# Preparing the first block of an attention and experts kernel in another order: normalization by tiles, transposes between two weight halves, scores ahead of values

## The chip, the cores and the metric

The kernel runs on one core of a Trainium2 chip. The metric is the device time of one execution in microseconds (us), lower is better. TensorE (PE; PEld is its weight load) multiplies and transposes into PSUM. VectorE (DVE), ScalarE (ACT) and GpSimd (POOL) do the elementwise work, and SyncE (SP) issues most DMAs. Each engine works through a queue of its own, and semaphores order the queues against each other.

## What is computed

One layer with pre-normalization, in float32, on x of 4096 tokens by 256 features:

```
z  = layernorm(x)
x  = x + softmax(causal((z Qw) (z Kw)^T / 16)) (z Vw)
z1 = layernorm(x);  h = z1 W_in + b_in
route = the best 2 of 8 experts by softmax(h W_gate + b_gate), shares summing to 1
x  = x + (sum over experts of route * (relu(h W1 + b1) W2 + b2)) W_out + b_out
```

An expert has 1024 hidden features.

## The kernel before

The tokens are 8 blocks of 512 (`TB`), each of 4 tiles of 128 rows (`TPB`). Queries go in groups of 256 (`QB`), two for each block, 16 in all; group g needs the keys and values of groups 0 to g.

`prepare_scores` turns Qw and Kw by transposes on TensorE and multiplies them (L406, in two halves `pqk0` and `pqk1`, one for each 128 features), so that scores are z (Qw Kw^T) z^T; VectorE scales each half into `qk_sb` (L413). `stats0(b)` takes mean and variance of the four x tiles of a block on VectorE (L231, L232) and calls `ln_rstd`, which on GpSimd adds epsilon and raises to the power -1/2 (L237, L238) for four columns, one for each tile, at once. `ln_rows` computes the four shifts in one VectorE instruction (L244) and then four normalized tiles z (L251). `turn` transposes the four tiles on TensorE (L262, 8 transposes of 128x128 into two PSUM tiles of 128x512) and VectorE copies each PSUM tile to SBUF (L263). `turn` serves the first norm (`turn(0, ...)`, result zT) and the second (`turn(1, ...)` in `enter`, result z1T).

`project(b)` multiplies zT by the combined weights (L426, `pq`, copied to qT by VectorE, L433), and then makes the values (L438, `pv`, copied by ScalarE, L445). `scores(g)` multiplies zT by qT for each key group (L468), keeps the scores in SBUF (ScalarE, L477) and a running maximum (VectorE, L483). The last key group is masked (L487), the maximum over the keys is formed through the tiles `top` (L493 to L498), transposes `pt` (L504), a reduction `m` (L506) and transposes `pmax` (L511). VectorE subtracts it (L515, L521) and ScalarE takes the exponential (L518, L524). `attend(g)` multiplies by the values (L533, `po`), divides, adds to x, and takes the statistics of the second norm. `enter(b)` runs the second norm's transposes, multiplies by W_in (L280, `ph`) and adds biases on VectorE (L287, L288). `route(b)` picks the experts. The experts' work follows from about 520 us on. `prepare_biases` transposes biases and W_in and folds the gate into W_in (L179 to L217).

PSUM tiles come from three rotating sets: `ps_mm` (4 buffers: pqk, pq, ps, ph), `ps_tr` (2 buffers: pt, pmax, pz, the weights' transposes) and `ps_o` (2 buffers: pv, po). A tile waits until its buffer's last readers are done.

The order on each engine comes from a scheduler that starts from the order of the text and the dependencies; `tc.keep_in_program_order` fixes instructions against each other, and `tc.issue_after(i)` lets what stands under it follow i. At the start the text reads:

```
    stats0(0)
    ready = prepare_scores()
    first_rows = ln_rows(0, 0, attn)
    with tc.issue_after(ready.ins):
        turn(0, 0, first_rows, zT[0])
    ready = project(0)
    with tc.issue_after(ready.ins):
        stats0(1)
```

Some setup follows, then `prepare_biases()`, `row = scores(0)`, and the loop over the groups. In pass g the loop computes `scores(g + 1)` ahead of `attend(g)`; on the first group of a block it also runs `enter` for the block before, turns the next block and projects it.

Of the kernel before, what the change touches and what calls it, by code (L numbers as in the profile page):

```python
# [17 lines left out]
P = 128  # L18
# [17 lines left out]
def preln_attention_moe_kernel(  # L36
# [18 lines left out]
    nc = tc.nc  # L55

    _, S, D = x.shape
    NE, _, FF = W1.shape
    NT = S // P
    NB = S // TB  # L60
    TPB = TB // P
# [29 lines left out]
    def ps_mm(name):  # L91
        return psum.tile([P, TB], F32, tag="mm", name=name, bufs=4)

    def ps_tr(name):
        return psum.tile([P, TB], F32, tag="tr", name=name, bufs=2)
# [15 lines left out]
    for _ in range(5):  # L111
        done = nc.tensor.matmul(
            pw[:, :QB],
            lhsT=zeros,
            rhs=zeros.unsqueeze(1).to_broadcast([P, QB // P, P]),
            start=True,
            stop=True,
        )
# [40 lines left out]
    ident = const.tile([P, P], F32, tag="ident", name="ident")  # L159
# [17 lines left out]
    def prepare_biases():  # L177
        ptb = ps_tr("pbias")
        nc.tensor.transpose(ptb[:, :NBR], brows, ident[:NBR, :NBR])  # L179
        biasT = const.tile([P, NBR], F32, tag="biasT", name="biasT")  # L180
        nc.scalar.copy(biasT, ptb[:, :NBR])
        nc.sync.dma_start(
            out=bias1.rearrange("(e p) f -> p e f", p=P),
            in_=biasT[:, : NE * NF].rearrange("p (e f) -> p e f", f=NF),
        )

        winT = piece("winT", ND, D)
        for k in range(ND):
            pt = ps_tr(f"pwin{k}")
            for c in range(ND):  # L190
                nc.tensor.transpose(pt[:, ts(c, P)], win_sb[:, c, ts(k, P)], ident)
            nc.scalar.copy(winT[:, k, :], pt[:, :D])
        for c in range(ND):
            pg = ps_o(f"pwg{c}")
            for k in range(ND):
                nc.tensor.matmul(
                    pg[:, :NE],
                    lhsT=winT[:, k, ts(c, P)],
                    rhs=wgate_sb[:, k, :],
                    start=(k == 0),  # L200
                    stop=(k == ND - 1),
                )
            nc.vector.tensor_copy(win_sb[:, c, D:], pg[:, :NE])
        binc = piece("binc", ND, P)
        nc.vector.tensor_copy(
            binc, biasT[:, NE * NF :].unsqueeze(2).to_broadcast([P, ND, P])
        )
        pg = ps_o("pbg")
        for k in range(ND):
            nc.tensor.matmul(  # L210
                pg[:, :NE],
                lhsT=binc[:, k, :],
                rhs=wgate_sb[:, k, :],
                start=(k == 0),
                stop=(k == ND - 1),
            )
        nc.vector.tensor_tensor(bgate_bc, pg[:, :NE], bgate_bc, ALU.add)  # L217
# [3 lines left out]
    lns = [  # L221
        tuple(
            const.tile([P, NT, w], F32, tag=f"ln{k}{s}", name=f"ln{k}{s}")
            for s, w in (("mv", 2), ("rstd", 1), ("shift", 1))
        )
        for k in range(2)
    ]
# [3 lines left out]
        nc.vector.bn_stats(out=st, in_=xb[t // TPB][:, t % TPB, :])  # L231
        nc.vector.bn_aggr(out=lns[k][0][:, t, :], in_=st)  # L232

    def ln_rstd(k, b):
        s = ts(b, TPB)
        mv, rstd, _ = lns[k]
        nc.gpsimd.tensor_scalar_add(rstd[:, s, 0], mv[:, s, 1], EPS)  # L237
        nc.gpsimd.tensor_tensor(rstd[:, s, 0], rstd[:, s, 0], half[:, s], ALU.pow)  # L238

    def ln_rows(k, b, pool):  # L240

        s = ts(b, TPB)
        mv, rstd, shift = lns[k]
        nc.vector.scalar_tensor_tensor(  # L244
            shift[:, s, :], mv[:, s, 0:1], -1.0, rstd[:, s, :], ALU.mult, ALU.mult
        )
        zs = []
        for j in range(TPB):
            t = b * TPB + j
            z = pool.tile([P, D], F32, tag=f"z{k}", name=f"z{k}_{t}", bufs=TPB)  # L250
            nc.vector.tensor_scalar(  # L251
                z, xb[b][:, j, :], rstd[:, t, :], shift[:, t, :], ALU.mult, ALU.add
            )
            zs.append(z)
        return zs

    def turn(k, b, zs, zT):

        for c in range(ND):
            pt = ps_tr(f"pz{k}_{b}_{c}")  # L260
            for j in range(TPB):
                nc.tensor.transpose(pt[:, ts(j, P)], zs[j][:, ts(c, P)], ident)  # L262
            nc.vector.tensor_copy(zT[:, c, :], pt)  # L263


    share = [const.tile([P, NT], F32, tag=f"share{k}", name=f"share{k}") for k in range(TOPK)]
# [114 lines left out]
    attn = ctx.enter_context(tc.tile_pool(name="attn", bufs=1))  # L381
# [5 lines left out]
    zT = [attn.tile([P, ND, TB], F32, tag="kt", name=f"zT{b}", bufs=KT) for b in range(NB)]  # L387
# [2 lines left out]
    qk_sb = attn.tile([P, ND, D], F32, tag="qk", name="qk")  # L390
    qT = {}

    def prepare_scores():

        wT = {}
        for name, w in (("qwT", qw_sb), ("kwT", kw_sb)):
            wT[name] = attn.tile([P, ND, D], F32, tag=name, name=name)
            pt = ps_tr(f"p{name}")
            for h in range(ND):
                for c in range(ND):  # L400
                    nc.tensor.transpose(pt[:, ts(h * ND + c, P)], w[:, c, ts(h, P)], ident)
            nc.scalar.copy(wT[name].rearrange("p h d -> p (h d)"), pt)
        for c in range(ND):
            pp = ps_mm(f"pqk{c}")
            for h in range(ND):
                done = nc.tensor.matmul(  # L406
                    pp[:, :D],
                    lhsT=wT["qwT"][:, h, ts(c, P)],
                    rhs=wT["kwT"][:, h, :],
                    start=(h == 0),  # L410
                    stop=(h == ND - 1),
                )
            nc.vector.tensor_scalar_mul(qk_sb[:, c, :], pp[:, :D], QSCALE)  # L413
        return done

    def stats0(b):
        for t in range(b * TPB, (b + 1) * TPB):
            ln_stats(0, t)
        ln_rstd(0, b)

    def project(b):
        qT[b] = attn.tile([P, ND, TB], F32, tag="qT", name=f"qT{b}", bufs=2)
        for o in range(ND):
            pp = ps_mm(f"pq{b}_{o}")
            for c in range(ND):
                nc.tensor.matmul(  # L426
                    pp,
                    lhsT=qk_sb[:, c, ts(o, P)],
                    rhs=zT[b][:, c, :],
                    start=(c == 0),  # L430
                    stop=(c == ND - 1),
                )
            done = nc.vector.tensor_copy(qT[b][:, o, :], pp)  # L433
        nc.gpsimd.memset(vb[b][:, :, D : D + 1], 1.0)
        for j in range(TPB):
            pv = ps_o(f"pv{b}_{j}")
            for c in range(ND):
                nc.tensor.matmul(  # L438
                    pv[:, :D],
                    lhsT=zT[b][:, c, ts(j, P)],  # L440
                    rhs=vw_sb[:, c, :],
                    start=(c == 0),
                    stop=(c == ND - 1),
                )
            nc.scalar.copy(vb[b][:, j, :D], pv[:, :D])  # L445
        return done


    KU = QB // P
# [469 lines left out]

    stats0(0)
    ready = prepare_scores()
    first_rows = ln_rows(0, 0, attn)
    with tc.issue_after(ready.ins):
        turn(0, 0, first_rows, zT[0])
    ready = project(0)
    with tc.issue_after(ready.ins):
        stats0(1)
# [6 lines left out]
    first = const.tile([P, TPB, NE], F32, tag="first", name="first")  # L936
# [23 lines left out]
        in_=zero.unsqueeze(1).to_broadcast([P, TOPK * (TPB + 1), D]),  # L960
    )

    prepare_biases()
    row = scores(0)
    for g in range(NT // KU):
        b, q = divmod(g, QPB)
        coming = q == 0 and b + 1 < NB
        lg = []

        def send():  # L970
            lg.append(enter(b - 1, rows1, attn))


        last = q == 0 and b == NB - 1
        nxt = None
        if g + 1 < NT // KU:
            nxt = scores(g + 1, send if last else None)
        if coming:
            ahead = ln_rows(0, b + 1, attn)
        if last:  # L980

            early = seen
            tables["a"] = plan("a", early, NFULL, SB, 0)
            seen = route(b - 1, lg[0], seen, attn)
            got, hTs = {}, {}
            for n in range(AHEAD + 1):
                got[n] = fetch_rows(work[n])
            for n in range(AHEAD):
                got[n] += fetch_weights(work[n])
            weighed = AHEAD  # L990
        elif q == 0 and b > 0:
            send()
        if coming:
            turn(0, b + 1, ahead, zT[b + 1])
        attend(g, row)
        row = nxt
        if coming:
            project(b + 1)
        if lg and not last:
            seen = route(b - 1, lg[0], seen, attn)  # L1000
        if q == QPB - 1:
            ln_rstd(1, b)
            if b + 2 < NB:
                stats0(b + 2)
            rows1 = ln_rows(1, b, attn)
# [172 lines left out]
```

## Time and profile before

| | us |
|---|---|
| median of 3 runs | 1099.73 |
| the runs | 1099.19 to 1102.57 |
| the profiled execution's own time | 1095.71 |
| its span in the trace | 1093.9 |

| engine | busy, us | share of the span |
|---|---|---|
| TensorE | 1079.7 | 99% |
| VectorE | 691.7 | 63% |
| ScalarE | 331.9 | 30% |
| GpSimd | 236.9 | 22% |

The profile is one execution; its times are from its own start. A timeline line gives start and length in us, the engine, the line of the kernel, the operation, the tile written and the tiles read, the shape, how many instructions were merged, and in brackets the idle time of the engine just before and what ended it. A matmul of float32 shows as two records in the trace. The length of a merged matmul line includes the end of the last one, so that the next line can begin before it is over. PEclk is the TensorE clock that was granted, as a share of full speed.

### The profile page before, as it was taken

Reading aid. Unit: us, or ns where it says so; the run is one execution under the profiler, and the core shown is the slowest. Engines: PE = TensorE matmul, PEld = TensorE weight load, DVE = VectorE, ACT = ScalarE, POOL = GpSimd, SP = SyncE. Lnnn points to the kernel's source line nnn. Section 1 sums busy time; section 2 is a strip of 40 time slices with the busy share of each in tenths; the row PEclk is TensorE's granted clock in tenths of the full one; section 3 lists DMA queues with packets and bytes.
Section 4 is the critical chain, followed back from the end, with each engine's and each line's share of the span. In section 5 each row is a group of like instructions: output and inputs, shape, how many; then the busy total and the mean of one; then the engine's idle time right before and its main releaser. Section 6 shows DMA issues by size and latency. Waiting matters only on the chain.

```text
span 1093.9 us, 15689 instructions
## 1 busy us (share of the span) xinstructions
PE 1079.7 (99%) x5077; PEld 896.3 (82%) x5077; DVE 691.7 (63%) x2132; ACT 331.9 (30%) x730; POOL 236.9 (22%) x286
## 2 busy tenths in 40 slices
PE   8999999999999999999999999999999999999998
PEld 6778888888888888888888888686878777777887
DVE  4677576574574555536393743867678876767636
ACT  1223232332341423223132122232322332324244
POOL 2023211212011110201222332323232231313110
PEclk9999999999999999999999999999999999999999
DMA  8010101001001000100075456797979796969285
GB/s 267 1 39 1 40 0 40 1 1 39 1 0 40 1 1 1 39 1 19 21 255 170 141 170 215 248 309 236 326 228 336 240 336 217 327 220 320 96 289 191
DMA packets 114888, 148.34 MB, mean 136 GB/s; under 512 B 23149, under 2 KB 94770, under 8 KB 114804
## 3 DMA queue, kind: packets, MB, share of 16 engines
q1 hardware_dynamic: 105876, 129.70, 36.1%
q0 software_dynamic: 8384, 17.09, 4.6%
q8 instruction: 41, 0.67, 0.3%
q14 instruction: 43, 0.35, 0.2%
q10 hardware_dynamic: 544, 0.52, 0.1%
HBM read 124.79 MB, written 22.75 MB: 135 GB/s over the span
## 4 chain that ended last, share of the span: by engine, by line
PE 95%; DVE 3%; DMA 1%; POOL 0%; issue 0%; ACT 0%; SPq 0%; ACTq 0%; DVEq 0%
PE po L533 20%; PE ps L468 19%; PE pm_a L827 11%; PE pe_a L894 11%; PE pe_b L894 5%; PE pm_b L827 5%; PE ph L280 3%; PE pq L426 3%; PE pm_c L857 3%; PE pf L1064 3%; PE pv L438 3%; PE pe_c L894 3%; PE pe_d L894 2%; PE pm_d L857 2%; PE pz L262 1%; PE pm_z L827 1%
## 5 line engine op out<-in xcount | busy, mean ns | idle before, releaser
L533 PE MATMUL po<-v,s 128*128 128x257 f32 x1056 | 238.3, 381 | 0.7 <-ACT s L524 0.7
L468 PE MATMUL ps<-qT,zT 128*128 128x256 f32 x1088 | 233.1, 374 | 0.0
L468 PEld LDWEIGHTS ps<-qT,zT 128*128 128x128 f32 x1088 | 203.4, 191 | 26.9 <-DVE mx L483 0.4
L533 PEld LDWEIGHTS po<-v,s 128*128 128x128 f32 x1056 | 197.3, 191 | 27.3 <-issue 1.6
L477 ACT COPY s<-ps 128x512 f32<-128x512 f32 x120 | 70.2, 585 | 193.3 <-PE ps L468 153.9
L894 PE MATMUL pe_a<-w_a,mid_a 128*128 128x256 f32 x544 | 121.6, 381 | 0.0
L827 PE MATMUL pm_a<-hT_a,w_a 128*128 128x256 f32 x544 | 120.0, 379 | 0.0
L483 DVE TENSOR_TENSOR mx<-ps,mx 128x512 f32<-128x512 f32 x91 | 62.8, 690 | 88.7 <-ACT s L477 88.2
L894 PEld LDWEIGHTS pe_a<-w_a,mid_a 128*128 128x128 f32 x544 | 102.9, 190 | 18.7 <-issue 5.4
L356 POOL DMA_INDIRECT slots<-assign,ati x64 | 62.6, 978 | 256.2 <-DVE ati L354 238.1
L827 PEld LDWEIGHTS pm_a<-hT_a,w_a 128*128 128x128 f32 x544 | 103.6, 190 | 13.8
L836 ACT ACTIVATE mid_a<-pm_a,c_a 128x256 f32<-128x256 f32 x136 | 64.2, 472 | 165.2 <-PE pm_a L827 157.8
L518 ACT ACTIVATE s<-s 128x512 f32<-128x512 f32 x120 | 72.0, 629 | 51.2 <-DVE s L515 51.2
L794 DVE STREAM_TRANSPOSE hT_a<-h_a 32x128 f32<-32x128 f32 x272 | 82.2, 302 | 3.8
L515 DVE TENSOR_TENSOR s<-s,pmax 128x512 f32<-128x512 f32 x120 | 73.1, 682 | 8.2 <-PE pmax L511 8.2
L903 POOL DMA_INDIRECT parts<-y_a,slot_a x34 | 34.2, 1005 | 162.5 <-DVE y_a L902 132.5
L794 DVE STREAM_TRANSPOSE mid_c<-raw_c 32x256 f32<-32x256 f32 x128 | 55.8, 436 | 1.9
L894 PE MATMUL pe_b<-w_b,mid_b 128*128 128x256 f32 x256 | 56.8, 380 | 0.0
L827 PE MATMUL pm_b<-hT_b,w_b 128*128 128x256 f32 x256 | 56.6, 379 | 0.0
L894 PEld LDWEIGHTS pe_b<-w_b,mid_b 128*128 128x128 f32 x256 | 48.6, 190 | 9.3 <-issue 2.6
L827 PEld LDWEIGHTS pm_b<-hT_b,w_b 128*128 128x128 f32 x256 | 48.8, 190 | 6.5
L836 ACT ACTIVATE mid_b<-pm_b,c_b 128x256 f32<-128x256 f32 x64 | 30.1, 471 | 63.0 <-PE pm_b L827 63.0
(279 smaller groups left out, 1209.5 us busy)
## 6 DMA issues: line engine op xcount, KB each, us to landing
w_a<-in_L_ffn_W_dram SPq DMA_DIRECT2D x68, 512.0 KB, 5.6
w_d<-in_L_ffn_W_dram SPq DMA_DIRECT2D x48, 512.0 KB, 7.2
w_c<-in_L_ffn_W_dram SPq DMA_DIRECT2D x32, 512.0 KB, 6.6
w_b<-in_L_ffn_W_dram SPq DMA_DIRECT2D x32, 512.0 KB, 6.5
rows<-hr SPq DMA_DIRECT2D x16, 512.0 KB, 4.1
yp<-parts SPq DMA_DIRECT2D x14, 512.0 KB, 8.5
x<-in_L_attn_x_dram SPq DMA_DIRECT2D x7, 512.0 KB, 6.5
out_dram<-ot SPq DMA_DIRECT2D x14, 256.0 KB, 4.0
```

The costliest lines, as they stand in the source:

```text
L356: put = nc.gpsimd.indirect_dma_start(out=slots, out_offset=bass.IndirectOffsetOnAxis(ap=ati[:, j : j + 1], axis=0), in_=assign[:, b * TPB ...
L468: nc.tensor.matmul(ps[:, u * QB + lo : (u + 1) * QB], lhsT=zT[kt // TPB][:, d, ts(kt % TPB, P)], rhs=qT[b][:, d, q * QB + lo : (q + 1) * Q ...
L477: nc.scalar.copy(flat, ps)
L483: nc.vector.tensor_tensor(mx, ps, old, ALU.max)
L515: nc.vector.tensor_tensor(s, s, pm[:, :QB].unsqueeze(1).to_broadcast([P, KU, QB]), ALU.subtract)
L518: nc.scalar.activation(s, s, AF.Exp)
L533: nc.tensor.matmul(po[u][:, : D + 1], lhsT=ss[c][:, k, ts(u, P)], rhs=vb[kt // TPB][:, kt % TPB, :], start=(kt == 0), stop=(kt == g * KU + u),
L794: nc.vector.transpose(to[ts(f, SQ)][..., ts(q, SQ)], of[ts(q, SQ)][..., ts(f, SQ)])
L827: nc.tensor.matmul(pm[:, :SB], lhsT=w1[c][:, ts(f, P)], rhs=hT[:, c, :], start=(c == 0), stop=(c == ND - 1),)
L836: nc.scalar.activation(mid[f // 2][:, f % 2, :], pm[:, :SB], AF.Relu, bias=c1[:, f : f + 1])
L857: nc.tensor.matmul(pm[ts(j, rest), :], lhsT=hT[:, c, ts(j, rest)], rhs=w1[c][:, ts(i, TB)], start=(c == 0), stop=(c == ND - 1),)
L894: nc.tensor.matmul(pe[ts(j, rest), :D], lhsT=mid[f][:, ts(u, P)][:, ts(j, rest)], rhs=w2[f // (NF // 2)][:, f % (NF // 2), :], start=(f == 0),
```

## The change

For the first block `ln_rstd` and `ln_shift` (the shift, now a function of its own) work on one tile at a time instead of four. `prepare_scores` takes a function `between` and calls it between its two halves; the first block's `turn` is given to it, with its transposes held in program order, and with ScalarE instead of VectorE copying the second PSUM tile. In `turn`, for every block and for both norms, the PSUM tile now comes from `ps_mm` and no longer from `ps_tr`. The values leave `project` for a function `values`; for the first block it is called after `scores(0)`, and `prepare_biases` after both. For the other blocks `values` directly follows `project`, as before.

```diff
--- before.py
+++ after.py
@@ -231,22 +231,28 @@
         nc.vector.bn_stats(out=st, in_=xb[t // TPB][:, t % TPB, :])
         nc.vector.bn_aggr(out=lns[k][0][:, t, :], in_=st)
 
-    def ln_rstd(k, b):
-        s = ts(b, TPB)
+    def ln_rstd(k, b, tiles=TPB):
+
+        s = ts(b, tiles)
         mv, rstd, _ = lns[k]
         nc.gpsimd.tensor_scalar_add(rstd[:, s, 0], mv[:, s, 1], EPS)
         nc.gpsimd.tensor_tensor(rstd[:, s, 0], rstd[:, s, 0], half[:, s], ALU.pow)
 
-    def ln_rows(k, b, pool):
-
-        s = ts(b, TPB)
+    def ln_shift(k, b, tiles=TPB):
+        s = ts(b, tiles)
         mv, rstd, shift = lns[k]
         nc.vector.scalar_tensor_tensor(
             shift[:, s, :], mv[:, s, 0:1], -1.0, rstd[:, s, :], ALU.mult, ALU.mult
         )
+
+    def ln_rows(k, b, pool, tiles=TPB):
+
+        mv, rstd, shift = lns[k]
         zs = []
         for j in range(TPB):
             t = b * TPB + j
+            if t % tiles == 0:
+                ln_shift(k, t // tiles, tiles)
             z = pool.tile([P, D], F32, tag=f"z{k}", name=f"z{k}_{t}", bufs=TPB)
             nc.vector.tensor_scalar(
                 z, xb[b][:, j, :], rstd[:, t, :], shift[:, t, :], ALU.mult, ALU.add
@@ -254,13 +260,18 @@
             zs.append(z)
         return zs
 
-    def turn(k, b, zs, zT):
+    def turn(k, b, zs, zT, first=False):
 
         for c in range(ND):
-            pt = ps_tr(f"pz{k}_{b}_{c}")
+            pt = ps_mm(f"pz{k}_{b}_{c}")
             for j in range(TPB):
-                nc.tensor.transpose(pt[:, ts(j, P)], zs[j][:, ts(c, P)], ident)
-            nc.vector.tensor_copy(zT[:, c, :], pt)
+                done = nc.tensor.transpose(pt[:, ts(j, P)], zs[j][:, ts(c, P)], ident)
+                if first:
+                    tc.keep_in_program_order(done)
+            if first and c:
+                nc.scalar.copy(zT[:, c, :], pt)
+            else:
+                nc.vector.tensor_copy(zT[:, c, :], pt)
 
 
     share = [const.tile([P, NT], F32, tag=f"share{k}", name=f"share{k}") for k in range(TOPK)]
@@ -390,7 +401,7 @@
     qk_sb = attn.tile([P, ND, D], F32, tag="qk", name="qk")
     qT = {}
 
-    def prepare_scores():
+    def prepare_scores(between):
 
         wT = {}
         for name, w in (("qwT", qw_sb), ("kwT", kw_sb)):
@@ -403,6 +414,8 @@
         for c in range(ND):
             pp = ps_mm(f"pqk{c}")
             for h in range(ND):
+                if c and not h:
+                    between()
                 done = nc.tensor.matmul(
                     pp[:, :D],
                     lhsT=wT["qwT"][:, h, ts(c, P)],
@@ -410,13 +423,14 @@
                     start=(h == 0),
                     stop=(h == ND - 1),
                 )
+                tc.keep_in_program_order(done)
             nc.vector.tensor_scalar_mul(qk_sb[:, c, :], pp[:, :D], QSCALE)
-        return done
-
-    def stats0(b):
+
+    def stats0(b, tiles=TPB):
         for t in range(b * TPB, (b + 1) * TPB):
             ln_stats(0, t)
-        ln_rstd(0, b)
+            if (t + 1) % tiles == 0:
+                ln_rstd(0, t // tiles, tiles)
 
     def project(b):
         qT[b] = attn.tile([P, ND, TB], F32, tag="qT", name=f"qT{b}", bufs=2)
@@ -431,6 +445,9 @@
                     stop=(c == ND - 1),
                 )
             done = nc.vector.tensor_copy(qT[b][:, o, :], pp)
+        return done
+
+    def values(b):
         nc.gpsimd.memset(vb[b][:, :, D : D + 1], 1.0)
         for j in range(TPB):
             pv = ps_o(f"pv{b}_{j}")
@@ -443,7 +460,6 @@
                     stop=(c == ND - 1),
                 )
             nc.scalar.copy(vb[b][:, j, :D], pv[:, :D])
-        return done
 
 
     KU = QB // P
@@ -919,11 +935,9 @@
 
 
 
-    stats0(0)
-    ready = prepare_scores()
-    first_rows = ln_rows(0, 0, attn)
-    with tc.issue_after(ready.ins):
-        turn(0, 0, first_rows, zT[0])
+    stats0(0, 1)
+    first_rows = ln_rows(0, 0, attn, 1)
+    prepare_scores(lambda: turn(0, 0, first_rows, zT[0], True))
     ready = project(0)
     with tc.issue_after(ready.ins):
         stats0(1)
@@ -960,8 +974,9 @@
         in_=zero.unsqueeze(1).to_broadcast([P, TOPK * (TPB + 1), D]),
     )
 
+    row = scores(0)
+    values(0)
     prepare_biases()
-    row = scores(0)
     for g in range(NT // KU):
         b, q = divmod(g, QPB)
         coming = q == 0 and b + 1 < NB
@@ -996,6 +1011,7 @@
         row = nxt
         if coming:
             project(b + 1)
+            values(b + 1)
         if lg and not last:
             seen = route(b - 1, lg[0], seen, attn)
         if q == QPB - 1:
```

## Prediction

> **What bounds the kernel now.** I read the head of the page, then the table by stage, then the instructions of TensorE in order of time, then the other engines around each hole.
>
> ```profile
> span 1093.9 us, 15689 instructions
> PE 1079.7 (99%) x5077; PEld 896.3 (82%) x5077; DVE 691.7 (63%) x2132; ACT 331.9 (30%) x730; POOL 236.9 (22%) x286
> ```
>
> TensorE is busy for 1079.7 of 1093.9 us. The change adds and removes no matmul, so it can only move TensorE's idle time, 14.2 us in all, and the time at half clock. The stage table says where these are (columns: stage, length, then busy time and count of PE, PEld, DVE, ACT, POOL, then the granted clock and DMA):
>
> ```profile
> 10.60:14.00 3.40, 1.67 (x8) 0.95 (x8) 3.11 (x8) 0.00 (x0) 2.81 (x38) 1.00 0.99 323
> 14.00:17.40 3.40, 3.17 (x4) 1.52 (x5) 0.77 (x2) 0.00 (x0) 0.00 (x0) 0.50 0.98 315
> 20.80:42.00 21.20, 19.05 (x97) 14.67 (x97) 13.03 (x44) 5.75 (x17) 1.28 (x2) 1.00 0.18 58
> 42.00:72.00 30.00, 27.28 (x136) 22.49 (x136) 24.17 (x72) 7.97 (x18) 5.03 (x5) 1.00 0.03 11
> 110.00:1040.00 930.00, 929.54 (x4363) 773.99 (x4362) 591.53 (x1843) 278.55 (x612) 209.36 (x211) 1.00 0.42 136
> ```
>
> From 110 to 1040 us there is half a microsecond of idleness: nothing to win, only to lose. What a start can give is 1.7 us before the first transposes, 2.2 us at 20.8 to 42, 2.7 us at 42 to 72, and the half clock of 14.0 to 17.4. The first chain, from the timeline:
>
> ```profile
> 8.03 2.00 PE L406 MATMUL pqk<-kwT,qwT 128*128 128x256 f32 x8 [0.67 <-ACT kwT L402]
> 8.64 0.43 DVE L231 BATCH_NORM_STATS2 bn<-x 128x6 f32<-128x256 f32 x1 [2.25 <-DMA x<-in_L_attn_x_dram]
> 9.38 0.23 POOL L237 TENSOR_SCALAR ln0rstd<-ln0mv 128x4 f32<-128x4 f32 x1 [7.46 <-DVE past L331]
> 9.78 1.04 POOL L238 TENSOR_TENSOR ln0rstd<-ln0rstd,half 128x4 f32<-128x4 f32 x1
> 11.06 1.86 DVE L251 TENSOR_SCALAR z<-x,ln0rstd,ln0shift 128x256 f32<-128x256 f32 x4
> 11.99 1.75 PE L262 MATMUL pz<-ident,z 128*128 128x128 f32 x8 [1.97 <-DVE z L251]
> 14.23 5.26 PE L426 MATMUL pq<-zT,qk 128*128 128x512 f32 x8 [0.49 <-DVE zT L263]
> ```
>
> The fourth x tile lands late (statistics at 8.64), and everything hangs on it: add, power, z, transposes, copies, pq at 14.23. The combined weights (L406) are finished in the hole before that and cost nothing. The later holes:
>
> ```profile
> 30.43 1.54 PE L533 MATMUL po<-v,s 128*128 128x257 f32 x6 [0.67 <-ACT s L524]
> 32.71 0.43 PE L511 MATMUL pmax<-ident,m 128*128 128x128 f32 x2 [0.52 <-DVE m L506]
> 34.54 0.63 PE L262 MATMUL pz<-ident,z 128*128 128x128 f32 x4 [0.97 <-DVE s L521]
> 60.66 0.33 PE L504 MATMUL pt<-ident,top 128*128 128x128 f32 x1 [1.52 <-DVE top L496]
> 65.22 0.63 PE L262 MATMUL pz<-ident,z 128*128 128x128 f32 x4 [0.85 <-DVE s L521]
> 105.77 0.66 PE L504 MATMUL pt<-ident,top 128*128 128x128 f32 x2 [0.44 <-DVE top L496]
> ```
>
> **Part 1, normalization by tiles: +0.4 us.** In GpSimd's built order the four one-column adds stand together, and then the four powers. The last add waits for the fourth tile, so no power starts before 9.78, as now: tile by tile exists in the text, not in the queue. DVE takes three shifts, three z, a shift, a z. What does a one-column power cost? Not in the trace. Below: a quarter of 1.04, 0.26. Above: all of it, 1.04. The add takes 0.23 for four columns, the power 0.81 more; I take 0.23 plus a quarter of 0.81, 0.43, as the add's row is the nearest fixed part. The third power then ends at 9.78 + 3 x 0.43 = 11.07 instead of 10.82, and the extra shift costs 0.16: the last z ends at 13.33 instead of 12.92. With 0.26 it is -0.1, with 1.04 the fourth power ends at 13.94 and the last z about 14.6, +1.7.
>
> **Part 2, half of the combined weights behind the transposes: +0.25.** The transposes end 0.41 later, about 13.99 (now 13.58). There stood a wait of 0.65 for the zT copy; now the second half of L406 stands there, four records of 0.215, 0.86 us. In the hole at 8.9 it was free, here it is on the path. It covers the first zT copy (0.68, DVE) and the second (ScalarE, 0.58 by its 128x512 copies), and its own scaling (0.37) hides behind the first pq matmul. So pq starts at 14.85, not 14.23: +0.62. If the half clock again lasts from 14.0 to 17.4, work of 0.86 + 3.44 starts at 13.99, 1.71 is done by 17.41, and pq ends at 20.0 instead of 19.33: +0.67. I take +0.65 for both parts.
>
> The trace gave half clock to 14.0-17.4, right after a stage of 3.4 us with only transposes. By the Trainium skill's page "TensorE: Matmul & The Clock Gate", Part 1, a window of about 3.4 us without activity brings the clock to half, and Part 4 says that transposes do not count as busy. This speaks against the change: it takes 0.86 us of matmuls out of 7.2-10.6 us, and with the gate shut a window earlier the last five transposes would take 0.21 us each, as at 5.5 us, not 0.11; the sum would then be 0.3 to 0.5 worse.
>
> **Part 3, scores before values: -1.2.** After pq (time E), TensorE holds the same work up to the scores of the third query group (42.04): 22.7 us from E = 19.33, of which 0.83 + 0.68 + 1.13 in the three holes above (start to start, less one record) and about 0.5 in small ones, so 19.5 of work. In the new order I follow the queues. The second qT copy ends at E+0.9; one pv matmul (0.43) covers it but for 0.1. DVE's queue then has statistics of block 1 before the first mask, so the mask starts at E+2.4 although the scores are there at E+2.0; top is copied by E+3.45, TensorE arrives at E+3.54. But the shift of block 1 stands before the last top, and waits for GpSimd: statistics E+2.75, add and power 1.35, shift to E+4.4, top E+4.6; pt stalls 0.57. Behind it three z of 0.34 and m 0.42: pmax at E+6.1 with the values done at E+5.62, 0.48 idle. The biases and the next scores then follow without a hole: exp and its ScalarE copies are ready 0.2 to 0.3 earlier each. At the second row pmax waits 0.35 behind two x updates. Sum 1.5 and 0.5 of small ones: 2.0 instead of 3.2. The bias write on SP goes out some 3 us later; SP's order is unchanged, and its reader is hundreds of us away.
>
> **Part 4, the transposes' PSUM pool: -0.75.** turn() now takes ps_mm for every block, both norms. The compiled order moves the z1 transposes ahead of the values at six of the blocks; the wait of L262 for s-pmax is the wait for a pair of ps_tr buffers. At 56.8-70.8: the transposes fill 57 to 57.9, but the wait for top until 60.66 stays, since DVE sets it (top alone took 2.00 us there). Then the 0.85 hole goes: ph starts from the first z1T copy at 63.0, three values cover the second, and pq starts near 69.75 + 0.1 instead of 70.84, -1.0. At 103.4 DVE is behind: the z1T copy ends at 105.7, ph waits 0.64 and again 0.15, against 0.6 now: +0.25. Later blocks, this example at 161.32:
>
> ```profile
> 161.32 1.90 PE L533 MATMUL po<-v,s 128*128 128x257 f32 x8
> 161.52 0.29 DVE L487 TENSOR_TENSOR s<-ps,mask 128x128 f32<-128x128 f32 x1
> 161.73 0.41 DVE L495 TENSOR_TENSOR top<-mx 128x256 f32<-128x256 f32 x1
> ```
>
> New order: eight transposes 0.88, two values 0.86, ph at +1.74. z1T's copy comes after L495, done at about +1.45: 0.3 of cover. Then top (+2.1) meets pt at +2.2, m meets pmax at +4.25. Zero each, if DVE is no more than 0.3 late. Values that used to cover these waits now come afterwards; without the cover each costs the copy, 0.6 to 0.7.
>
> **Sum.** 0.65 - 1.2 - 1.0 + 0.25 = -1.3 us. The profiled execution took 1095.71 us (span 1093.9 and 1.8 around it), the median of the runs is 1099.73, 4.0 above. So 1094.4 for a profiled one, 1098.4 for the median. Power bounds: -1.8 to 0.
>
> **Rivals.** (a) Faster by over 0.3% (3.3 us, about what a measurement of this kernel tells from no change). The half clock costs 3.4 x 0.5 = 1.7 us; if the new run escapes it and powers cost 0.26: -1.3 - 1.7 - 0.5 = -3.5, 1096.2. For it: fewer holes. Against: 10.6-14 holds only transposes again. (b) Slower: ph behind the z1T copies. At five blocks ph, pt and pmax now follow their DVE steps with little between. If DVE arrives later than those 0.3 us, each block pays two copies and m, 0.69 + 0.69 + 0.42 = 1.8: with the -1.0 lost too, 0.65 - 1.2 + 5 x 1.8 = +8.5, 1108.2. It passes 3.3 us from 0.8 us a block. For it: 930 us without idleness cannot improve, and at 103.4 DVE was 0.8 late. Against: at 161, 232 and 317 us DVE starts the mask 0.20 us after the last score, each time. (c) The text changes and the time does not: the powers cost 1.04, parts 1 and 3 cancel, 0.0, 1099.7.
>
> **Numbers.** Forecast 0.50, (c) 0.14, (a) 0.22, (b) 0.14. Forecast and (c) lie within 0.3%: 0.64; faster 0.22; slower 0.14. The range takes in (a) and the power's bound with the runs' spread (1099.19 to 1102.57): 1095.4 to 1101.8.
>
> **What would show it.** Four adds, then four powers of 0.3 to 0.6 after the last add; last z near 13.3; L406's second half after the transposes; pq starting 14.6 to 15.8, later than now; holes at pt and pmax (about 0.5 each) while values run; the third group's scores near 41.5; the 0.85 wait gone at 65; no new wait of ph over 0.3 after 110 us. Powers that start before 9.3, or ph waits of 1 us at 161 and on, prove me wrong.

## Result and the profile after

| | median, us | runs | lowest to highest |
|---|---|---|---|
| before | 1099.18 | 22 | 1097.36 to 1102.57 |
| changed | 1097.91 | 22 | 1095.04 to 1100.16 |

The ratio of the changed kernel to before is 0.9992, 95% interval 0.9984 to 0.9999: 1.3 us less by the medians, 0.1 to 1.8 by the interval, within 0.3%. The forecast was 1.3 us less. The size came out right, but most of its terms were wrong, so that the agreement is luck.

The profiled execution took 1100.16 us, the longest of the 22. The head of the page, and the table by stage with the columns of before:

```profile
span 1098.4 us, 15700 instructions
PE 1080.9 (98%) x5077; PEld 894.7 (81%) x5077; DVE 689.2 (63%) x2134; ACT 331.9 (30%) x731; POOL 238.1 (22%) x292
```

```profile
10.60:14.00 3.40, 1.86 (x6) 1.10 (x7) 3.01 (x8) 0.00 (x0) 2.88 (x40) 0.61 1.09 350
14.00:17.40 3.40, 3.40 (x10) 2.53 (x9) 1.04 (x2) 0.58 (x1) 0.00 (x0) 0.50 1.08 346
17.40:20.80 3.40, 3.40 (x8) 1.45 (x8) 0.69 (x1) 0.00 (x0) 0.00 (x0) 0.89 1.10 369
20.80:42.00 21.20, 20.94 (x107) 15.96 (x107) 13.44 (x46) 6.60 (x19) 1.28 (x2) 1.00 0.15 44
42.00:72.00 30.00, 28.41 (x137) 22.59 (x136) 24.77 (x75) 7.63 (x17) 5.04 (x5) 1.00 0.10 33
110.00:1040.00 930.00, 925.31 (x4331) 768.32 (x4330) 587.83 (x1836) 277.99 (x612) 208.13 (x210) 1.00 0.42 136
```

Read against before: TensorE's idle time in 20.8 to 42 us went from 2.2 to 0.3 us, in 42 to 72 from 2.7 to 1.6. Between 110 and 1040 us there are 4.7 idle us where there was half a microsecond. And the half clock, once 14.0 to 17.4 alone, now begins at 11.32 and lasts to 18.15, two windows of 3.41 us. The first chain, from the timeline:

```profile
7.33 1.13 PE L419 MATMUL pqk<-kwT,qwT 128*128 128x256 f32 x4 [0.73 <-ACT kwT L413]
8.00 0.43 DVE L231 BATCH_NORM_STATS2 bn<-x 128x6 f32<-128x256 f32 x1 [1.56 <-DMA x<-in_L_attn_x_dram]
8.73 0.21 POOL L238 TENSOR_SCALAR ln0rstd<-ln0mv 128x1 f32<-128x1 f32 x1 [2.00 <-DVE past L342]
9.05 2.18 POOL L239 TENSOR_TENSOR ln0rstd<-ln0rstd,half 128x1 f32<-128x1 f32 x4
11.24 0.44 PE L268 MATMUL pz<-ident,z 128*128 128x128 f32 x1 [2.79 <-DVE z L257]
12.74 0.62 DVE L257 TENSOR_SCALAR z<-x,ln0rstd,ln0shift 128x256 f32<-128x256 f32 x1
14.53 1.92 PE L419 MATMUL pqk<-kwT,qwT 128*128 128x256 f32 x4
16.24 4.55 PE L440 MATMUL pq<-zT,qk 128*128 128x512 f32 x8
```

The fourth add (8.73) waits for the fourth tile; all four powers stand behind it and take 2.18 us in a row. The last z ends at 13.36. The second half of the combined weights runs behind the transposes and at half clock, 0.43 us a record. Then pq starts at 16.24; before it was 14.23. The stage of block 1:

```profile
31.76 1.04 PE L268 MATMUL pz<-ident,z 128*128 128x128 f32 x8
32.63 1.47 PE L549 MATMUL po<-v,s 128*128 128x257 f32 x6
33.94 0.27 PE L520 MATMUL pt<-ident,top 128*128 128x128 f32 x1
34.05 1.02 PE L440 MATMUL pq<-zT,qk 128*128 128x512 f32 x2
34.91 0.27 PE L520 MATMUL pt<-ident,top 128*128 128x128 f32 x1
35.88 0.38 PE L527 MATMUL pmax<-ident,m 128*128 128x128 f32 x2
```

No bracket is left. Before, the order was po, pt, pmax, pz, pq, with waits of 0.67, 0.52 and 0.97 us among them. Now the eight transposes of block 1 stand ahead of po, and pq's matmuls stand between the two pt and pmax. Later lines, among them the stage at 161 us and the two holes that make up the loss after 110 us:

```profile
59.89 0.33 PE L520 MATMUL pt<-ident,top 128*128 128x128 f32 x1 [1.25 <-DVE top L512]
104.67 0.71 PE L291 MATMUL ph<-win,z1T 128*128 128x264 f32 x2 [0.40 <-DVE z1T L274]
160.78 1.04 PE L268 MATMUL pz<-ident,z 128*128 128x128 f32 x8
161.65 1.03 PE L549 MATMUL po<-v,s 128*128 128x257 f32 x4
162.52 0.61 PE L291 MATMUL ph<-win,z1T 128*128 128x264 f32 x2
560.31 1.98 PE L549 MATMUL po<-v,s 128*128 128x257 f32 x8 [1.09 <-DVE rinv L559]
635.39 5.41 PE L843 MATMUL pm_a<-hT_a,w_a 128*128 128x256 f32 x16 [2.85 <-ACT mid_a L852]
```

The top wait at 60 stays, ph at 162 waits for nothing, ph at 104 waits 0.40. The holes at 560 and 635, and the half clock of 3.41 us that follows the second, are in none of the twelve later traces. They go far to explain why this execution is the longest. Whether other runs of this comparison have them is not known, since they left no trace.

### The profile page after: what moved, and what is told of

Same layout as the page of the kernel before. It is cut to its first block, busy times and chain, and to the rows that moved or that the text cites. A ratio compares the mean times of both kernels' runs of the same rounds, so it can differ in the third digit from the quotient of the medians.

```text
span 1098.4 us, 15700 instructions
## 1 busy us (share of the span) xinstructions
PE 1080.9 (98%) x5077; PEld 894.7 (81%) x5077; DVE 689.2 (63%) x2134; ACT 331.9 (30%) x731; POOL 238.1 (22%) x292
## 5 line engine op out<-in xcount | busy, mean ns | idle before, releaser
L910 PE MATMUL pe_b<-w_b,mid_b 128*128 128x256 f32 x256 | 56.8, 380 | 0.0
```

The source lines that it names most:

```text
L910: nc.tensor.matmul(pe[ts(j, rest), :D], lhsT=mid[f][:, ts(u, P)][:, ts(j, rest)], rhs=w2[f // (NF // 2)][:, f % (NF // 2), :], start=(f == 0),
```

## The markers, and the kernels by them

The experiments ran in three groups (e1 to e4, e5 to e8, e9 to e12), each on one chip beside before, which takes 1091.8 us there; so ratios and markers in the traces are compared, not times with those above. Why the same kernels took 6 to 7 us more in the first comparison (before 1099.18, the changed kernel at full clock 1095.38) is open, and the granted clock of before's 22 runs there is not known. In what follows the experts start with the first `pm_a` (582.6 us in e5). The markers:

- **Norm:** from the start of the fourth x tile's statistics to the end of the last z.
- **Gap:** the longest stretch between the warm-up (the matmuls on zeros, L112) and block 0's pq, from the start of one multiplication on TensorE to the start of the next, transposes not counted; and how many windows of 3.41 us at half clock follow.
- **Row:** from the first matmul behind block 0's pq to the first pq of block 2. Half clock inside it (once, 1.7 us) is taken out.
- **Full-clock median:** of the runs without any half clock, and how many these are. A window at half clock lowers a run's mean granted clock by 3.41 x 0.5 / 1090 = 0.0016, so the list of the runs shows their number: 1.000, 0.998, 0.997, 0.995.

| kernel | norm | gap, windows | row | full-clock median | ratio to before (95%) |
|---|---|---|---|---|---|
| before | 4.28 | 4.59, 1 | 51.51 | 1091.78 (19 of 24) | 1 |
| changed, first profile | 5.36 | 6.46, 2 | 48.33 | 1095.38 (2 of 22) | 0.9992 (0.9984 to 0.9999) |
| e1 pool only | 4.24 | 5.95, 2 | 47.75 | none of 12 | 0.9984 (0.9975 to 0.9993) |
| e2 old pool | 5.32 | 4.83, 1 | 52.69 | none of 8 | 1.0038 (1.0025 to 1.0051) |
| e3 one power | 4.24 | 4.31, 1 | 48.32 | 1087.79 (4 of 7) | 0.9962 (0.9947 to 0.9976) |
| e4 halves together | 5.32 | 3.59, 1 | 48.33 | 1088.79 (3 of 12) | 0.9983 (0.9972 to 0.9994) |
| e5 changed again | 5.31 | 4.84, 1 | 48.32 | 1089.09 (2 of 11) | 0.9989 (0.9980 to 0.9999) |
| e6 scores first only | 4.21 | 2.69, 0 | 52.71 | 1092.98 (2 of 6) | 1.0031 (1.0019 to 1.0043) |
| e7 order and pool | 4.21 | 2.94, 0 | 48.32 | 1087.72 (4 of 7) | 0.9974 (0.9963 to 0.9985) |
| e8 tile by tile | 2.74 | 4.29, 2 | 48.31 | none of 11 | 0.9991 (0.9982 to 1.0000) |
| e9 values, then scores | 5.32 | 4.80, 1 | 48.27 | 1088.74 (2 of 9) | 0.9979 (0.9968 to 0.9990) |
| e10 fed | 5.33 | 2.38, 0 | 48.34 | 1091.45 (11 of 11) | 0.9991 (0.9982 to 1.0000) |
| e11 powers in turn | 3.13 | 2.67, 0 | 48.33 | 1087.08 (5 of 5) | 0.9953 (0.9939 to 0.9967) |
| e12 pairs | 3.28 | 2.34, 0 | 48.33 | 1088.02 (5 of 5) | 0.9953 (0.9938 to 0.9967) |

The norm and gap of before are from the first profile, where the fourth tile's statistics began at 8.64 us. In the experiments this landing was mostly near 6.4, sometimes 8.0; its luck is part of the spread. The full-clock median of before is that of the second group, where 3 of 24 runs have 0.998 and 2 have 0.999; in the others it is 1091.82 and 1091.76.

## Experiments

### The PSUM pool: e1, e2

e1 is before with part 4 alone, e2 the changed kernel without it:

```diff
-            pt = ps_tr(f"pz{k}_{b}_{c}")
+            pt = ps_mm(f"pz{k}_{b}_{c}")
```

> The kernel before with one line changed: the turned block's PSUM tiles come from the pool of two that the matrix products use. My theory (the pool takes away the wait in front of block 2's pq): pq of blocks 0 and 1 starts as before (14.2 and 35.1 us), pq of block 2 about 1.0 us earlier (69.8), pq of block 3 about 0.75 earlier (0.25 given back at the ph behind it), and the time about 0.75 us less, a ratio near 0.9993. Rival, the pool does nothing and block 2 gained only by the earlier scores: every marker as before to 0.3 us, the time the same. Rival, ph waits behind the copies in every block: each later block loses 0.5 to 1 us more, pq of block 7 is 3 to 5 us late.

("The pool of two" is a slip: `ps_mm` has four buffers, `ps_tr` two.)

> The changed kernel with the turned block's PSUM tiles from their old pool again. My theory: pq of blocks 0 and 1 starts as in the changed kernel (16.2 and 34.0 us), pq of block 2 about 1.0 us later than there (69.9 against 68.95), pq of block 3 about 0.75 later, the time 0.75 us more than the changed kernel's, and thus no gain left against before. Rival, the pool does nothing: block 2's pq stays at 69.0 and the time is the changed kernel's.

In e2 the row grows from 48.32 to 52.69, by 4.4 us, where I expected 1.0. From block 1's pq to block 2's it is 0.88 once its half clock is taken out, as expected; the other 3.5 us lie ahead of block 1's pq, where I had expected nothing. The same holes as in before are back, here in e6, which has the old pool too:

```profile
28.43 0.77 PE L506 MATMUL pt<-ident,top 128*128 128x128 f32 x2 [0.53 <-DVE top L498]
29.86 0.43 PE L513 MATMUL pmax<-ident,m 128*128 128x128 f32 x2 [0.66 <-DVE m L508]
31.69 0.63 PE L262 MATMUL pz<-ident,z 128*128 128x128 f32 x4 [0.96 <-DVE s L523]
```

The second half of pz waits for the `ps_tr` buffer of pmax to be read (s), pt and pmax wait for VectorE, and pq, which could cover all three, waits for pz. In `ps_mm` pz takes other buffers and goes ahead of po, and pq fills the waits. e2 shows a second cost: 4.68 us without a multiplication there (30.50 to 35.18) was followed by a half-clock window at 35.55. (e6 has the same 4.68 and no window in its profile; 4 of its 6 runs have one.)

e1 is not the clean part that I took it for. With `ps_tr` free, the scheduler also put the first bias transpose in front of the combined weights, where TensorE waited for a DMA:

```profile
10.87 0.34 PE L179 MATMUL pbias<-ident,brows 66*128 66x66 f32 x1 [4.22 <-DMA brows<-in_L_ffn_b_dram]
11.01 3.72 PE L406 MATMUL pqk<-kwT,qwT 128*128 128x256 f32 x8
```

All its 12 runs have half clock, and it still beats before. Its row of 47.75 lacks 0.57 us of bias work done earlier; with that it is 48.32.

### The order of scores and values: e6, e9

e6 is before with part 3 alone; e9 is the changed kernel with the two calls exchanged (`values(0)` ahead of `row = scores(0)`, `prepare_biases()` behind both):

```diff
-    prepare_biases()
     row = scores(0)
+    values(0)
+    prepare_biases()
...
             project(b + 1)
+            values(b + 1)
```

> The kernel before with only the first scores put ahead of the first values. My theory on record: the row of idle between the first scores and block 1's pq shrinks by 1.2 us, so from the end of block 0's pq to block 1's pq it is 14.5 us where before has 15.72. Rival, which the run with the old pool speaks for (16.91 us there against 13.42): the gain in this stage is the PSUM pool's alone, scores first costs 1.2 us without it, because the second group's pt, pmax and pz then wait with nothing between them: 16.9 us, and the time 1 to 3 us over before.

> The changed kernel with the first values in front of the first scores again; the PSUM pool and the rest stay. Theory (with the new pool the wait is gone whichever comes first): from the end of block 0's pq to block 1's pq within 0.5 us of the changed kernel's 13.42, so scores first is worth next to nothing with the pool and costs 1.17 without it (16.89 against 15.72). Rival, my forecast, scores first is worth 1.2 us: 14.6 us here. Later blocks as in the changed kernel in both.

e6's row is 52.71, 1.2 over before's 51.51, and at full clock it is 1.2 us slower (1092.98 against 1091.78). e9's row is 48.27, 0.05 less than the changed kernel's. (From pq's end to block 1's pq alone e9 has 11.50, but only because pq moved ahead of po and the last bias product; block 2's pq is where it was.) So the order is worth nothing in the row with the new pool, and costs 1.2 us without it. (At full clock e9's median is 0.35 us under e5's, but these are two runs each.) My forecast of -1.2 had the wrong sign on the old pool.

### The start: e3, e4, e5, e7

e3 undoes part 1, e4 undoes the place of the transposes, e7 does both, e5 is the changed kernel again.

```diff
-    stats0(0, 1)
-    first_rows = ln_rows(0, 0, attn, 1)
+    stats0(0)
+    first_rows = ln_rows(0, 0, attn)
```

```diff
             for h in range(ND):
-                if c and not h:
-                    between()
...
             nc.vector.tensor_scalar_mul(qk_sb[:, c, :], pp[:, :D], QSCALE)
+        between()
```

> The changed kernel with the first block's statistics finished for four tiles at once (one add and one power of 128x4), the rest of the change kept. My theory (four powers on the same queue behind four adds take 2.2 us in a row where one takes 1.04): the power starts when the fourth tile's statistics are there (about 8.9 to 9.2 us), ends about 1.1 us earlier than the last of the four, the last z lies 0.5 to 1.1 us earlier than 13.36, and block 0's pq starts 0.5 to 1.1 us earlier than 16.24, twice that if the gate leaves the clock full. Rival, tiles one by one are no loss, since VectorE rows and transposes run beside the powers: last z and pq within 0.3 us of the changed kernel's.

> The changed kernel with both halves of the scores' combined weights ahead of the transposes, as before. My theory (the second half, 0.86 us at full and 1.92 us at half clock, lies on the path behind the last transpose): pq of block 0 starts 0.9 us earlier than 16.24 if only the place counts, and up to 1.9 us earlier if the second half runs in front of the gap at full clock. Rival, the clock's gate is the cost: the two slow windows (11.3 to 18.2 us) come whatever the place, and pq ends within 0.4 us of 20.6; with one slow window only, as before, pq ends 1.2 us or more earlier.

> The changed kernel itself, unaltered, for a comparison with the others on one chip. Theory (what a run costs is set at the start: last landing of x to last z 5.36 us, and how many windows of the clock are shut behind the hole): end of block 0's pq to start of block 1's pq 13.42 us as in the first profile; no hole of 1.47 us at 559 us and none of 3.2 us at 632 us, which were that one execution's; time then 4 us under the first profile's 1100.2 for the same number of shut windows. Rival, these two holes belong to the changed kernel: both come again and the part after the attention takes 510.6 us, not 505.9.

> The changed kernel with the normalization of the first block undone (one power for four tiles, both halves of the combined weights ahead of the transposes), so scores first and the PSUM pool alone. Theory: last landing of x to last z 4.25 us where the changed kernel takes 5.36; block 0's pq 2 us earlier than the changed kernel's for the same landing; 13.42 us from the end of pq to block 1's pq; later blocks as in the changed kernel; mostly no shut window; time 2 to 4 us under the changed kernel, ratio to before near 0.9965. Rival, the tile-wise start pays by early transposes: the time is that of the changed kernel or more.

Normalization by tiles costs 1.1 us: norm is 5.31 to 5.36 in the kernels that have four powers behind four adds, 4.21 to 4.28 in those with one power. At full clock e3 is 1.3 us under e5 (before's full-clock medians beside them differ by 0.04).

In e4 pq started at 13.15 against 14.60 in e5, for the same landing, but the half clock came later, over pq (13.61 to 17.02, in e5 11.09 to 14.50), and pq ended at 18.38, in e5 at 18.03. The first line is e4's, the second e5's:

```profile
13.15 5.40 PE L439 MATMUL pq<-zT,qk 128*128 128x512 f32 x8 [0.49 <-DVE zT L274]
14.60 3.60 PE L440 MATMUL pq<-zT,qk 128*128 128x512 f32 x8
```

The rival was right for the clock: the window comes in both and takes the gain. At full clock e4 is 0.3 us under e5.

e5 has row 48.32, 505.9 us behind the start of the experts, as before, and no hole at 559 or 632: the rival fell.

e7 keeps parts 3 and 4 alone. At full clock it is 4.06 us under before, and 1.37 under the changed kernel. It comes out of the traces: row -3.19, and from block 2's pq to the experts 516.28 us instead of 517.17, -0.89; the sum is -4.08.

### The clock: e10

```diff
+    def warm_and_turn():
+        feed(6)
+        turn(0, 0, first_rows, zT[0], True)
...
                 done = nc.tensor.transpose(pt[:, ts(j, P)], zs[j][:, ts(c, P)], ident)
+                    if c == 0:
+                        feed({0: 4, 2: 3}.get(j, 0))
```

> The changed kernel with 13 matmuls of 128x256 on zeros set into PE's wait of the start: six behind the first half of the combined weights, four behind the first transpose, three behind the third. Their product is used by nothing. Theory (the shut windows come from this wait): no window at half clock behind it, the second half of the combined weights at 0.21 us each and not 0.43, end of pq about 16 to 16.5 us for a landing near 6.4 where the changed kernel has 18.0, nearly all runs at the clock 1.0, median 1.5 to 2 us under the changed kernel's (ratio to before near 0.997 on a chip like the last). Rival, the clock follows something else (the start of the program, the power of other work): windows as often as in the changed kernel, and the time up to 0.5 us longer for the added work.

All 11 runs have the clock at 1.000, within 0.7 us of each other: the windows come from the wait. Its stage table, and the timeline:

```profile
10.60:14.00 3.40, 3.40 (x19) 2.94 (x18) 1.51 (x5) 0.00 (x0) 1.34 (x13) 1.00 1.09 349
14.00:17.40 3.40, 3.40 (x16) 2.25 (x15) 1.12 (x2) 0.59 (x1) 0.00 (x0) 1.00 1.09 347
```

```profile
11.11 1.89 PE L946 MATMUL warm<-zeros 128*128 128x256 f32 x8
14.36 0.71 PE L268 MATMUL pz<-ident,z 128*128 128x128 f32 x5
14.90 1.03 PE L421 MATMUL pqk<-kwT,qwT 128*128 128x256 f32 x4
15.77 3.60 PE L442 MATMUL pq<-zT,qk 128*128 128x512 f32 x8
```

The time did not fall. I counted 13 matmuls as 13 records; a float32 matmul is two, and 26 records of 0.21 us filled more than the wait: the first transpose ran at 11.0 though z 0 was there near 9.6, and pq ended at 19.20, not at 16 to 16.5. The run shows the cause of the half clock, and no gain. It also gives the price of part 2 at full clock: from the last transpose to pq 0.97 us (14.80 to 15.77), where e7 has 0.76 (11.15 to 11.91): 0.21.

### Ways out: e8, e11, e12

e11 is the changed kernel with one order altered on GpSimd:

```diff
             if (t + 1) % tiles == 0:
-                ln_rstd(0, t // tiles, tiles)
+                with tc.issue_after(power.ins) if power else nullcontext():
+                    power = ln_rstd(0, t // tiles, tiles)
...
+    with tc.issue_after(power.ins):
         before = const.tile([P, P], F32, tag="before", name="before")
...
```

> The changed kernel with the tile-wise start made so that no tile waits for the next: each power issued ahead of the next tile's add, the statistics of tiles 2 and 3 behind the z of earlier tiles, transposes of each tile when its z is there, both zT copies side by side. Theory (four powers behind four adds are the loss of the tile-wise start): last landing of x to last z 2.4 to 3 us where the changed kernel takes 5.36, first z near 7 us, pq of block 0 starts at 11 to 12.5 us, no hole of PE over 2 us before it, mostly no shut window; time 1 us or more under the run with one power and both halves together, ratio to before 0.995 to 0.996. Rival, the short operations on GpSimd and VectorE cost as much as the waits they replace: last z within 0.5 us of the run with one power.

> The changed kernel with the order on GpSimd alone altered: each tile's power ahead of the next tile's add, the setup of masks and ranks behind the last power. Theory (the four adds in front of the four powers tie every tile to the last landing): first power near 4.9 us, last landing of x to last z 3 us or less instead of 5.31, block 0's pq 1.5 us or more earlier than the changed kernel's for the same landing. Rival, the powers themselves are the length: last landing to last z 4.5 us or more.

> A candidate: scores first and the pool as in the changed kernel, the first block normalized in two pairs of tiles, each pair's power (128x2) ahead of the next pair's add, z 0 and 1 ahead of the second pair's shift, transposes of a pair behind each half of the combined weights, both zT copies side by side. Theory: a power of 128x2 takes 0.65 to 0.75 us, last landing to last z 2.7 to 3.2 us where one power gives 4.21 and the changed kernel 5.31; block 0's pq starts near 10.7 us for a landing near 6.4, no hole of PE over 1.2 us, nearly all runs without a shut window; 1 us or more under the kernel with order and pool alone, ratio to before near 0.996. Rival, as with tile by tile: PE waits on the later z as long as before, shut windows come, 1090 us, ratio 0.999.

In e8 I also put the statistics of the last tile behind the third z (`with tc.issue_after(behind_row[1].ins)` around `ln_stats`). The norm is only 2.74, but it starts at 9.28 instead of about 6.4: VectorE waited for the third power first. Gap 4.29, two windows, no run at full clock. The theory was right on the powers and wrong on the time; my order on VectorE made a new wait.

e11 leaves VectorE alone. GpSimd's and VectorE's lines of its start:

```profile
4.83 0.58 POOL L239 TENSOR_TENSOR ln0rstd<-ln0rstd,half 128x1 f32<-128x1 f32 x1
5.71 0.58 POOL L239 TENSOR_TENSOR ln0rstd<-ln0rstd,half 128x1 f32<-128x1 f32 x1
6.75 0.43 DVE L231 BATCH_NORM_STATS2 bn<-x 128x6 f32<-128x256 f32 x1 [0.32 <-DMA x<-in_L_attn_x_dram]
6.82 0.57 POOL L239 TENSOR_TENSOR ln0rstd<-ln0rstd,half 128x1 f32<-128x1 f32 x1
7.79 0.60 POOL L239 TENSOR_TENSOR ln0rstd<-ln0rstd,half 128x1 f32<-128x1 f32 x1
8.49 1.39 DVE L257 TENSOR_SCALAR z<-x,ln0rstd,ln0shift 128x256 f32<-128x256 f32 x2
```

The first two powers are done before the last tile lands, the third runs beside that tile's statistics, only the fourth is left behind them, and norm is 3.13. pq starts at 11.41, where e5 has 14.60 for a landing 0.26 earlier. The gap is 2.67, all five runs are at full clock: 1087.08 us, 0.47% under before. e12 (powers of 128x2, 0.72 to 0.74 us) has the same ratio; its landing in the profile was 8.12 and it still had no window. **Both are faster than before and than the changed kernel** (0.9939 to 0.9967 and 0.9938 to 0.9967 against 0.9980 to 0.9999, on another chip). That they are faster than e3 or e7 is not shown: these intervals overlap.

## Why the prediction was right, and where it was wrong

The accounts, in us, predicted and measured:

| term | predicted | measured | from |
|---|---|---|---|
| part 1, norm by tiles | +0.4 | +1.1 | norm 5.31 against 4.21 |
| part 2, second half behind the transposes | +0.25 | +0.2 | 0.97 against 0.76 |
| the clock, at the start | 0 | +1.4 | what is left of the medians, see below |
| part 3, scores first | -1.2 | 0 (+1.2 alone) | e9, e6 |
| part 4, up to block 1's pq | 0 | -2.3 | 15.72 to 13.42, parts 3 and 4 |
| part 4, at 56.8 to 70.8 | -1.0 | -0.9 | 35.78 to 34.90 |
| part 4, later | +0.25 | -0.9 | 517.17 to 516.28 |
| sum | -1.3 | -1.4 | medians -1.3 |

That the sums agree is luck: part 1, the clock and part 3 came out 0.7, 1.4 and 1.2 dearer than forecast, and part 4 some 3.3 cheaper. The check of the measured terms is the sum without the clock, -2.8 from the traces, against -2.7 between the full-clock medians.

**Part 1.** Right: four adds, then four powers, none before the last landing. The power was mis-sized, 0.52 from start to start and not 0.43 (the bounds held it), so the third ended 1.62 us after the first began, not 1.29. And I let the z follow without loss: from the third shift to the last z took 2.65 us, where one shift and four z took 2.06. Together about 1.1. The last z at 13.36, near my 13.33, was luck: the landing was 0.64 us earlier.

**Part 2** held, at full clock. At half clock these four records take 1.7 us (14.53 to 16.24 in the changed kernel's first profile), which belongs to the next step.

**The clock.** I counted the half clock as unchanged, one window, and put the rule that speaks against this into a side sentence. The traces show this: of the starts in the table, those with a gap up to 2.94 us had no window, those from 3.59 on had one or two. The change makes the gap longer. For a landing near 6.4 it is 2.94 with neither part 1 nor part 2 (e7), 3.59 with part 1 (e4) and 4.84 with both (e5); in the first two profiles it grows from 4.59 to 6.46, from one window to two.

What a window costs can be read between the last z and the first matmul behind pq. At full clock that is 4.85 us (e7), and 5.06 with the 0.21 of part 2. In before it is 6.41, so its window cost 1.6; in e4 6.54, 1.7; in e5 6.23, 1.2; in the first profile of the changed kernel 7.27, 2.2 for two. It is less where part of the window falls ahead of the last z, when TensorE waits anyway (e5's begins at 11.09, the last z ends at 11.80). So in the first two profiles the clock took 0.65 us, a little over the 0.3 to 0.5 of my side sentence. That pq started at 16.24, outside the 14.6 to 15.8 that I had named, comes from it.

In the second group the clock took more, because 19 of 24 runs of before had no window and 9 of 11 of the changed kernel one or two: full-clock medians differ by 1091.78 - 1089.09 = 2.7 us, all medians by 1.3, and 1.4 is left for the clock.

The Trainium skill says it in "TensorE: Matmul & The Clock Gate", Part 1 and Part 4: a free-running window of about 3.4 us without activity halves the clock, and transposes do not count as busy in the same way. Before's window from 10.59 to 14.00, with eight transposes and no multiplication, agrees. Other windows here were not empty: e8's from 8.38 to 11.79 held 0.9 us of multiplications and half clock followed, e12's from 8.20 to 11.61 held as much and none followed. No run here shows the exact share of a window that keeps the clock full.

**Part 3** is the step that failed. The holes at pt and pmax while the values run stood where I had put them, but were half as long: 24.69 to 25.21 is 0.52 from start to start, 0.31 less one record, where I had 0.57, and at pmax 0.49 is 0.27, where I had 0.48. But I let the three later holes vanish because exp and its copies come earlier. They stay (e6: 0.53, 0.66, 0.96) until the pool is changed too (e5: none of them).

**Part 4** is the term that carries the gain, and I gave it nothing at block 1, though the line of 34.54 in the prediction's own list, pz waiting 0.97 for s, is the very wait that I named for `ps_tr` at 65 us. At 56.8 to 70.8 it held. At 103.4 I expected ph to lose 0.25; ph waits 0.40 there, but from block 2's pq to block 3's the kernel gained 0.29 (47.63 to 47.34 in e5). Then three blocks gained 0.2 each, one lost 0.27, and the last stretch gained 0.28, where I had zero.

**The rivals.** (a) needed both an escape from the half clock and cheap powers: neither came, though 2 of 22 runs escaped and lie at 1095.0 and 1095.7. (b) fell: ph waits for nothing at 162 us, and its longest wait behind 110 us is 0.22 (at 512, as in before). (c) is near in size, and a costlier start did cancel part of the gain, but part 3 had none to cancel.

## What to carry over

When a tile changes its PSUM pool, go through every wait on the old pool's rotation, the first block's too, and ask what work of the same engine now fills the neighbouring waits; that was worth some 4 us here, where the one wait that I had named is 0.9. Splitting a step into tiles brings nothing while one engine's queue still runs all first steps ahead of all second steps; read the built order, and tie the order (e11) before you count on it. Measure the longest stretch between multiplications before moving one, since here a stretch of 3.6 us or more in the start brought one or two windows at half clock, of 1.2 to 1.7 us each in four starts.

## What the runs showed that I had not expected

- GpSimd's power has a high fixed part: 0.54 to 0.60 us for 128x1, 0.72 to 0.74 for 128x2, 1.04 to 1.18 for 128x4.
- A 128x256 z on VectorE, 0.41 us alone, took 1.0 to 1.1 us where GpSimd ran its setup beside it (e11: 1.03, e5: 1.09), and 0.78 to 0.92 in other starts. What in that setup slows it was not tried.
- The fourth x tile landed near 6.4 us in most traces and at 8.0 to 8.6 in four, in kernels with the same loads. Why is open.
